# Choosing per sequence which states' dt*u*B TensorE makes, and issuing a step's two scans together

## The chip, the cores and the metric

The kernel runs on one core of a Trainium2 chip. Its time is the time that the device takes for one launch, in microseconds. The core has five engines that run side by side, each with its own queue of instructions: TensorE (PE in the profile; its weight loads are listed apart as PEld), VectorE (DVE), ScalarE (ACT), GpSimd (POOL) and SyncE (SP, which issues most of the DMAs here). All data is float32.

## What is computed

Two layers are applied to 16 sequences of 512 tokens with 256 channels. The first is a bidirectional selective state space layer with a residual and a layer norm; the second is a mixture of experts with soft slots (16 experts of 64 slots), again with a residual and a layer norm. The change touches the first only. Cut to what matters, with 512 inner channels and 16 states:

```python
xr = x @ in_proj_w.T                       # x part and gate "res"
xf = silu(causal_conv(xf));  xb = silu(causal_conv_b(xf))
# for each direction: delta (softplus), B and C come from u = xf or xb
dA = einsum('bld,dn->bldn', dt, A)
dB_u = einsum('bld,bld,bln->bldn', dt, u, B)          # dt*u*B
dA_cum = exp(reversed cumulative sum of the shifted dA)
xs = cumsum(dB_u * dA_cum, 1) / (dA_cum + 1e-12)
y = einsum('bldn,bln->bld', xs, C) + u * D            # times silu(res)
out = (y + y_b) @ out_proj_w.T
```

The kernel computes the running sum as a first order recurrence, h = exp(dt*A) * h + dt*u*B, and puts the division by (dA_cum + 1e-12) into a factor 1 + tanh(...). So for each sequence, direction, channel and state n there are: a product dt*u*B_n, a decay exp(dt*A_n), a tanh factor, one scan over the 512 positions, the product of scan and factor, and the product with C_n, summed over n.

## The kernel before, in words

The 512 inner channels stand on partitions as four chunks of 128; a tile is 128 channels by 512 positions. `seq_layers` goes through the sequences b. Each has four calls of `scan_part(b, r, p, ...)`: direction r (0 forward, 1 backward) and pair of chunks p, in the order (0,0), (1,0), (0,1), (1,1). A part walks through the 16 states two at a time (n and n+1) and for each through its two chunks. One state pair of one chunk is called a step here: 16 steps per part, 64 per sequence, 1,024 in all.

In a step:

- POOL makes `db` = du * B for the two states (line 427), from `du` = dt*u and from `bs`, two rows of B that a DMA spreads over all partitions (line 416).
- ACT writes exp(dt*A) into a PSUM bank `h` (line 444) and the tanh factor into `th` (line 446), for each of the two states.
- DVE scans in place in `h` (lines 450 and 452) and multiplies by (1 + `th`) into one half of `hg` (line 455).
- POOL multiplies `hg` by `cs`, the spread rows of C (line 456).
- PE adds `hg` into an accumulator by transposing it (`add_up`, line 371), two steps later.

For the states in DIAG, before the change 5 and 13, PE makes the product instead of POOL. `project_unit` writes the row of B_n onto the diagonals of four 128 by 128 blocks in DRAM (`diag_dram`, line 297, issued by ACT), with four clearing writes of `blank` at the start (line 188). `scan_part` loads those blocks as `dg` (line 420, on SP, a single buffer), `turn_pair` transposes `du` into `duT` once per part (lines 350 and 355), and `by_diagonal` multiplies the two into a PSUM bank `hd` (line 405), one step ahead of its use. Such a step has k = 1: `bs` and `db` hold one state only, and the decay of the other goes to `dec` in SBUF.

These buffers are small rings: `h` three banks, `th` three, `db` three, `bs` and `cs` three, `hg` four, `dec` two, and three further PSUM banks for everything else that PE does (`bank`), `hd` included.

Work beside the scan is cut into pieces by generators, held in three queues: `prep` (the next part's projections and step sizes: `pin`, `px`, `pz`, `pres`, `pdu`), `front` (finishing the former sequence and its dispatch to the slots: `pyt`, `po`, `pl`, `pd`, `pq`) and `back` (the experts of two sequences, `pg`, `pu`, `peo`, and `combine`, `cl`, `ctp`, `cpo`). `back` gets work from sequence 3 on, in the odd sequences, spread over 128 steps; in the last one over 64. After each step `beside_scan` lets the queues issue pieces, as long as no more than three banks are in use: `diags` holds the count of banks at each waiting `hd`, and `piece` stops when the count since the oldest one is over `BANKS`. `paced_piece` gives front and back a credit per step. What is left of front is issued at a sequence's end (`front.drain`, line 1023), what is left of back after the last sequence (`side_by_side`).

The order in which an engine's instructions stand in its queue is made by a planner when the program is built: of the instructions whose inputs and buffers it expects to be ready, it takes the one that comes first in the program. Instructions wrapped in `late` keep their place in the program's order.

Of the kernel before, what the change touches and what calls it, by code (L numbers as in the profile page):

```python
# [12 lines left out]
ALU = mybir.AluOpType  # L13
# [4 lines left out]
P = 128  # L18
# [6 lines left out]
NS = 16  # L25
DTR = 16
XB, XC = 32, 64
XW = XC + NS
KW = 4
NE = 16  # L30
DIAG = (5, 13)
DIAG_SIZE = P * (P + 1)
SL = 64
NSL = NE * SL
# [21 lines left out]
def seq_layers(tc, ident, neghalf, a, out):  # L56
# [20 lines left out]
    nc = tc.nc  # L77
    nb = a["x"].shape[0]
    with ExitStack() as ctx:
# [6 lines left out]
        diag_dram = drams.tile([2, len(DIAG), NL, DIAG_SIZE], F32, name="diag_dram")  # L86
# [176 lines left out]
        def prep_gate(b, fwd, out):  # L263
# [8 lines left out]
                late(nc.vector.scalar_tensor_tensor(res[:, c, :], res[:, c, :], 1.0, pp, ALU.add, ALU.mult))  # L272
            out["res"] = res

        def project_unit(b, r, out):

            w = side[r]
            q = f"{b}_{r}"
            yield GAP + 1
            px = bank(f"px_{q}")  # L280
            for c in range(ND):
                nc.tensor.matmul(
                    px[:XW, :], w["xT"][:, c, :], out["u"][:, c, :], start=(c == 0), stop=(c == ND - 1)
                )
            yield HOLD
            xd = p1.tile([XW, L], F32, tag=f"xd_{r}", name=f"xd_{q}")
            bc = dram.tile([2, NS, L], F32, tag="bc", name=f"bc_{q}")
            if r == 0:
                late(nc.scalar.activation(xd, px[:XW, :], AF.Identity, bias=unit))
            else:  # L290

                late(nc.scalar.activation(xd[: XB + NS, :], px[: XB + NS, :], AF.Identity, bias=unit[: XB + NS]))
                nc.scalar.copy(xd[XC:XW, :], px[XC:XW, ::-1])
            nc.sync.dma_start(bc[0], xd[XB : XB + NS, :])
            nc.sync.dma_start(bc[1], xd[XC:XW, :])
            step = DIAG[1] - DIAG[0]
            nc.scalar.dma_start(
                diag_dram[r].rearrange("i l (p s) -> i l p s", p=P)[:, :, :, 0],
                xd[XB + DIAG[0] : XB + NS : step, :].rearrange("i (l p) -> i l p", p=P),
            )  # L300
            out.update(xd=xd, bc=bc)

        def prep_pair(b, r, p, v):
# [88 lines left out]
        def scan_part(b, r, p, v, accs, done, then):  # L392

            prep.drain()
            prep.gens += [[1, g] for g in [turn_pair(b, r, p, v)] + then]
            w = side[r]
            made = {}

            def by_diagonal(n, c):

                diags.append(count[0])
                made[n, c] = h = bank(f"hd_{b}_{r}_{n}_{c}")
                for lc in range(NL):
                    s = slice(lc * P, (lc + 1) * P)
                    ins = nc.tensor.matmul(h[:, s], v[c][3][:, s], dg[:, s], start=True, stop=True)  # L405
                    if lc == 0:
                        late(ins)

            chunks = (2 * p, 2 * p + 1)
            for n in range(0, NS, 2):  # L410
                q = f"{b}_{r}_{p}_{n}"
                k = 1 if n + 1 in DIAG else 2

                bs = p4.tile([P, 2, L], F32, tag="bs", name=f"bs_{q}")
                cs = p4.tile([P, 2, L], F32, tag="cs", name=f"cs_{q}")
                nc.sync.dma_start(bs[:, :k, :], v["bc"][0, n : n + k, :].unsqueeze(0).to_broadcast([P, k, L]))
                nc.sync.dma_start(cs, v["bc"][1, n : n + 2, :].unsqueeze(0).to_broadcast([P, 2, L]))
                if n + 3 in DIAG:
                    dg = p4.tile([P, L], F32, tag="dg", name=f"dg_{q}", bufs=1)
                    nc.sync.dma_start(  # L420
                        dg.rearrange("p (l s) -> p l s", l=NL),
                        diag_dram[r, DIAG.index(n + 3), :, : P * P].rearrange("l (p s) -> p l s", p=P),
                    )
                for c in chunks:
                    dt, rr, du = v[c][:3]
                    db = p4.tile([P, 2, L], F32, tag="db", name=f"db_{q}_{c}")
                    nc.gpsimd.tensor_tensor(  # L427
                        db[:, :k, :], du.unsqueeze(1).to_broadcast([P, k, L]), bs[:, :k, :], ALU.mult
                    )
                    hg = p4.tile([P, 2, L], F32, tag="hg", name=f"hg_{q}_{c}", bufs=4)  # L430
                    hs = {}
                    for j in range(2):
                        if j < k:
                            dec = h = ps_h.tile([P, L], F32, tag="h", name=f"h_{q}_{c}_{j}")
                            hs[j] = (h, dec, db[:, j, :])
                        else:
                            h = made.pop((n + j, c))
                            dec = p4.tile([P, L], F32, tag="dec", name=f"dec_{q}_{c}", bufs=2)
                            hs[j] = (h, dec, h)

                    ths = {}
                    for j in range(2) if k == 2 else (1, 0):
                        s = slice(n + j, n + j + 1)
                        nc.scalar.activation(hs[j][1], dt, AF.Exp, scale=w["A"][:, c, s])  # L444
                        ths[j] = p4.tile([P, L], F32, tag="th", name=f"th_{q}_{c}_{j}")
                        nc.scalar.activation(ths[j], rr, AF.Tanh, bias=LN_1E12 / 2, scale=w["Ah"][:, c, s])  # L446
                    for j in range(2):
                        (h, dec, add), th = hs[j], ths[j]
                        if r == 0:
                            nc.vector.tensor_tensor_scan(h, dec, add, 0.0, ALU.mult, ALU.add)  # L450
                        else:
                            nc.vector.tensor_tensor_scan(  # L452
                                h[:, ::-1], dec[:, ::-1], add[:, ::-1], 0.0, ALU.mult, ALU.add
                            )
                        nc.vector.scalar_tensor_tensor(hg[:, j, :], th, 1.0, h, ALU.add, ALU.mult)  # L455
                    nc.gpsimd.tensor_tensor(hg, hg, cs, ALU.mult)  # L456
                    pending.append(
                        (r == n == 0, n == 0, r == 1 and n == NS - 2, c, hg, accs, w, v["u"], f"acc_{q}_{c}", done)
                    )
                    evict()  # L460

                    nxt_n = n if c == chunks[0] else n + 2
                    if nxt_n + 1 in DIAG:
                        for x in sides:
                            x.take_up()
                        by_diagonal(nxt_n + 1, chunks[1] if c == chunks[0] else chunks[0])
                    beside_scan()
                    if k == 1:
                        diags.pop(0)
                    add_up(2)  # L470
# [68 lines left out]
        prep, front, back = sides = [Side(), Side(), Side()]  # L539
# [556 lines left out]
```

## Time and profile before

| | us |
|---|---|
| median of 3 runs | 5415.38 (5413.15 to 5421.7) |
| the profiled execution | 5411.23 |
| its span, first to last instruction | 5409.4 |
| POOL busy | 4732.1 (87%) |
| DVE busy | 4559.7 (84%) |
| PE busy | 4331.1 (80%) |
| ACT busy | 4087.2 (76%) |
| first `hg` of the first sequence starts | 51.4 |
| last `hg` of the last sequence ends | 5132.3 |

Busy time is the time in which an engine executed at least one instruction; register and semaphore instructions and the issuing of DMAs are not counted. In a group's line of the profile stand the line of the kernel, the engine, the operation, what it writes and reads with shapes, the number of instructions; then their busy time and the mean of one in ns; then the idle time of the engine just ahead of them and what ended it. In a line of waits stand who waited for whom, the microseconds in all, how often, and the longest. A timeline's line has the start, the length, the engine and the instruction, and in brackets the idle time before it.

### The profile page before, as it was taken

The numbers are of one execution on the slowest core, as the hardware profiler recorded it, in microseconds if no ns is written. First come the engines' busy times: TensorE is split into PE (matmuls) and PEld (weight loads), VectorE is DVE, ScalarE is ACT, GpSimd is POOL, SyncE is SP. The second block draws the span as 40 slices with busy tenths as digits, with TensorE's granted clock in tenths as the row PEclk, the third lists the DMA queues.
The fourth block names the chain that finished last, engine by engine and source line by source line (L and its number), as shares of the span: only waits on it lengthen the run. The fifth ranks groups of instructions, "written<-read, shape, count | busy, mean of one in ns | idle before, by whom it ended". The sixth has DMA issues, their size and how long they took to land. (4 is left out here: it accounts for less than half of the span.)

```text
span 5409.4 us, 73721 instructions
## 1 busy us (share of the span) xinstructions
PE 4331.1 (80%) x24144; PEld 3390.0 (63%) x24145; DVE 4559.7 (84%) x6276; ACT 4087.2 (76%) x6515; POOL 4732.1 (87%) x2537
## 2 busy tenths in 40 slices
PE   5656666898888978788888977889787897888889
PEld 3445555676666666677656765667656776667657
DVE  7888988889898899888998888988899889988722
ACT  6677777787888778887877887788788887877641
POOL 6999999999999899998999989998999989988600
PEclk7778778898899988899888989899889998989999
DMA  4334333575446644566446754467444764457436
GB/s 137 131 117 137 125 129 131 189 230 159 156 142 212 225 149 148 158 223 213 131 144 194 232 170 153 132 212 232 149 149 146 225 224 134 145 179 234 126 103 188
DMA packets 595236, 907.73 MB, mean 168 GB/s; under 512 B 78082, under 2 KB 384898, under 8 KB 594852
## 3 DMA queue, kind: packets, MB, share of 16 engines
q1 hardware_dynamic: 521156, 859.87, 49.5%
q10 hardware_dynamic: 73696, 43.14, 2.8%
q8 instruction: 192, 3.15, 0.2%
q14 instruction: 192, 1.57, 0.1%
HBM read 840.86 MB, written 62.01 MB: 167 GB/s over the span
## 5 line engine op out<-in xcount | busy, mean ns | idle before, releaser
L456 POOL TENSOR_TENSOR hg<-hg,cs 128x1024 f32<-128x1024 f32 x1024 | 2420.8, 2368 | 128.1 <-DVE hg L455 110.0
L427 POOL TENSOR_TENSOR db<-du,bs 128x1024 f32<-128x1024 f32 (+1 forms) x1024 | 2144.4, 2098 | 232.3 <-DVE h L450 84.7
L371 PE MATMUL acc<-ident,hg 128*128 128x128 f32 x8192 | 1179.3, 295 | 203.3 <-POOL hg L456 181.6
L455 DVE SCALAR_TENSOR_TENSOR hg<-th,h 128x512 f32<-128x512 f32 x1792 | 1185.8, 678 | 177.2 <-PE acc L371 90.4
L371 PEld LDWEIGHTS acc<-ident,hg 128*128 128x128 f32 x8192 | 1044.9, 154 | 390.8 <-POOL hg L456 240.9
L452 DVE TENSOR_TENSOR_SCAN h<-h,db 128x512 f32<-128x512 f32 x896 | 1072.8, 1218 | 112.2 <-ACT h L444 107.5
L450 DVE TENSOR_TENSOR_SCAN h<-h,db 128x512 f32<-128x512 f32 x896 | 1071.1, 1217 | 48.8 <-ACT h L444 45.7
L446 ACT ACTIVATE th<-rr,Ah_f 128x512 f32<-128x512 f32 x1024 | 725.0, 714 | 186.3 <-DVE hg L455 183.1
L446 ACT ACTIVATE th<-rr,Ah_b 128x512 f32<-128x512 f32 x1024 | 721.5, 712 | 155.2 <-DVE hg L455 147.7
L444 ACT ACTIVATE h<-dt,A_f 128x512 f32<-128x512 f32 x896 | 608.2, 680 | 117.5 <-DVE hg L455 112.6
L444 ACT ACTIVATE h<-dt,A_b 128x512 f32<-128x512 f32 x896 | 608.6, 681 | 108.8 <-DVE hg L455 105.1
L687 PE MATMUL pl<-x2T,seT 128*128 128x512 f32 x512 | 299.1, 715 | 78.7 <-DVE hg L455 37.4
L405 PE MATMUL hd<-dg,duT 128*128 128x128 f32 x2048 | 305.6, 298 | 32.7 <-ACT yt L627 13.5
L830 PEld LDWEIGHTS pg<-st,Wg 128*128 128x128 f32 x2048 | 244.8, 196 | 106.2 <-issue 85.0
L405 PEld LDWEIGHTS hd<-dg,duT 128*128 128x128 f32 x2048 | 283.1, 214 | 38.4 <-ACT yt L627 15.7
L806 PE MATMUL peo<-Wd,ht 128*128 128x256 f32 x1024 | 257.0, 407 | 55.6 <-DVE rr L337 38.6
L779 PE MATMUL pu<-st,Wu 128*128 128x128 f32 x2048 | 254.5, 283 | 50.1 <-DMA Wu<-in_Wu_dram 32.7
L962 PE MATMUL cpo<-ceo,ct 128*128 128x256 f32 x1024 | 254.8, 407 | 46.9 <-DVE rr L337 39.9
L779 PEld LDWEIGHTS pu<-st,Wu 128*128 128x128 f32 x2048 | 244.9, 198 | 61.5 <-DVE h L452 24.2
L830 PE MATMUL pg<-st,Wg 128*128 128x128 f32 x2048 | 269.9, 286 | 4.1 <-DMA Wg<-in_Wg_dram 3.1
L884 PE MATMUL cl<-seT,cx 128*128 128x512 f32 x512 | 244.7, 617 | 32.5 <-DVE res L272 12.3
L806 PEld LDWEIGHTS peo<-Wd,ht 128*128 128x128 f32 x1024 | 205.3, 206 | 97.7 <-DVE rr L337 41.2
(154 smaller groups left out, 6654.8 us busy)
## 6 DMA issues: line engine op xcount, KB each, us to landing
cs<-bc SPq DMA_DIRECT2D x512, 512.0 KB, 3.9
bs<-bc SPq DMA_DIRECT2D x384, 512.0 KB, 5.1
Wg<-in_Wg_dram SPq DMA_DIRECT2D x128, 512.0 KB, 6.0
Wu<-in_Wu_dram SPq DMA_DIRECT2D x128, 512.0 KB, 6.0
Wd<-in_Wd_dram SPq DMA_DIRECT2D x128, 512.0 KB, 5.5
dg<-diag_dram SPq DMA_DIRECT2D x128, 256.0 KB, 4.2
bs<-bc SPq DMA_DIRECT2D x128, 256.0 KB, 3.6
x<-in_x_dram SPq DMA_DIRECT2D x32, 512.0 KB, 6.3
```

The source lines that it names most:

```text
L371: ins = nc.tensor.matmul(accs[c][:, s], hc[:, j, s], ident, is_transpose=True, start=False, stop=(last and j == 1 and lc == NL - 1),)
L405: ins = nc.tensor.matmul(h[:, s], v[c][3][:, s], dg[:, s], start=True, stop=True)
L427: nc.gpsimd.tensor_tensor(db[:, :k, :], du.unsqueeze(1).to_broadcast([P, k, L]), bs[:, :k, :], ALU.mult)
L444: nc.scalar.activation(hs[j][1], dt, AF.Exp, scale=w["A"][:, c, s])
L446: nc.scalar.activation(ths[j], rr, AF.Tanh, bias=LN_1E12 / 2, scale=w["Ah"][:, c, s])
L450: nc.vector.tensor_tensor_scan(h, dec, add, 0.0, ALU.mult, ALU.add)
L452: nc.vector.tensor_tensor_scan(h[:, ::-1], dec[:, ::-1], add[:, ::-1], 0.0, ALU.mult, ALU.add)
L455: nc.vector.scalar_tensor_tensor(hg[:, j, :], th, 1.0, h, ALU.add, ALU.mult)
L456: nc.gpsimd.tensor_tensor(hg, hg, cs, ALU.mult)
L779: nc.tensor.matmul(pu[:, fc * P : (fc + 1) * P], got["Wu", e][:, k, fc * P : (fc + 1) * P], st[:, k, :, j * SL : (j + 1) * SL], start=(k = ...
L806: nc.tensor.matmul(po[:, j * DM : (j + 1) * DM], ht[:, fc, :], got["Wd", e0 + j][:, fc, :], start=(fc == 0), stop=(fc == NF - 1),)
L830: nc.tensor.matmul(pg[:, fc * P : (fc + 1) * P], got["Wg", e][:, k, fc * P : (fc + 1) * P], st[:, k, :, j * SL : (j + 1) * SL], start=Fals ...
```

## The change

A function `diag_of(b)` chooses the states by sequence: 3, 7, 11 and 15 in sequences 0 to 2, states 3 and 11 in sequences 3 to 14, none in sequence 15. Everything that asked for DIAG asks for it now: the diagonal write, the load of `dg`, `by_diagonal`, and `turn_pair`, which is left out where there are no such states. `diag_dram` has room for four states, so eight clearing writes are issued at the start in place of four. Since state n+1 = 3 is in the second pair, `dg` is loaded in the first pair of a part (it was the second pair). Apart from that, the loop that issued scan, product, scan, product for the two states of a step issues scan, scan, product, product.

```diff
-DIAG = (5, 13)
+DIAG = (3, 7, 11, 15)
...
+        def diag_of(b):
+
+            return DIAG if b < 3 else DIAG[::2] if b + 1 < nb else ()
...
-            step = DIAG[1] - DIAG[0]
-            nc.scalar.dma_start(
-                diag_dram[r].rearrange("i l (p s) -> i l p s", p=P)[:, :, :, 0],
-                xd[XB + DIAG[0] : XB + NS : step, :].rearrange("i (l p) -> i l p", p=P),
-            )
+            ds = diag_of(b)
+            if ds:
+                step = ds[1] - ds[0]
+                own = diag_dram[r, DIAG.index(ds[0]) :: DIAG.index(ds[1]) - DIAG.index(ds[0])]
+                nc.scalar.dma_start(
+                    own.rearrange("i l (p s) -> i l p s", p=P)[:, :, :, 0],
+                    xd[XB + ds[0] : XB + NS : step, :].rearrange("i (l p) -> i l p", p=P),
+                )
...
-            prep.gens += [[1, g] for g in [turn_pair(b, r, p, v)] + then]
+            ds = diag_of(b)
+            prep.gens += [[1, g] for g in ([turn_pair(b, r, p, v)] if ds else []) + then]
...
-                k = 1 if n + 1 in DIAG else 2
+                k = 1 if n + 1 in ds else 2
...
-                if n + 3 in DIAG:
+                if n + 3 in ds:
...
                     for j in range(2):
-                        (h, dec, add), th = hs[j], ths[j]
+                        h, dec, add = hs[j]
                         if r == 0:
                             nc.vector.tensor_tensor_scan(h, dec, add, 0.0, ALU.mult, ALU.add)
...
-                        nc.vector.scalar_tensor_tensor(hg[:, j, :], th, 1.0, h, ALU.add, ALU.mult)
+                    for j in range(2):
+                        nc.vector.scalar_tensor_tensor(hg[:, j, :], ths[j], 1.0, hs[j][0], ALU.add, ALU.mult)
...
-                    if nxt_n + 1 in DIAG:
+                    if nxt_n + 1 in ds:
```

## The prediction

> **What bounds the kernel now.** I read the page's busy shares first, then the same shares in 40 slices of the span.
>
> ```profile
> PE 4331.1 (80%) x24144; PEld 3390.0 (63%) x24145; DVE 4559.7 (84%) x6276; ACT 4087.2 (76%) x6515; POOL 4732.1 (87%) x2537
> ...
> PE   5656666898888978788888977889787897888889
> ...
> POOL 6999999999999899998999989998999989988600
> ```
>
> POOL leads nearly everywhere; PE has room in the first seven slices only. The kernel has several regimes, so I cut it: 64 products `hg` (line 456, POOL) per sequence mark the borders. The view of busy time by window, for sequences 1, 4, 5, 15 and for what follows the scans:
>
> ```profile
> core 0: us, PE busy (x) PEld busy (x) DVE busy (x) ACT busy (x) POOL busy (x), PEclk, DMA share, GB/s
> ...
> 352.00:651.00 299.00, 200.59 (x1046) 158.39 (x1044) 262.67 (x322) 226.30 (x360) 292.70 (x153) 0.81 0.40 130
> ...
> 1276.00:1584.00 308.00, 244.41 (x1283) 185.28 (x1283) 282.13 (x384) 248.70 (x417) 295.27 (x157) 0.88 0.45 140
> 1584.00:1914.00 330.00, 285.01 (x1735) 230.51 (x1734) 283.77 (x398) 261.14 (x397) 294.92 (x156) 0.93 0.66 211
> ...
> 4765.00:5132.00 367.00, 310.76 (x1816) 248.85 (x1815) 282.35 (x414) 263.26 (x412) 285.22 (x150) 0.92 0.59 188
> 5132.00:5409.00 277.00, 248.69 (x1249) 185.01 (x1248) 67.52 (x191) 77.30 (x153) 14.96 (x45) 0.97 0.46 142
> ```
>
> Sequences 0 to 2 (301, 299, 300 us) are POOL's: 98% busy. From 3 on, POOL's work is the same, but its idle time grows with PE's load: 6 us at 201 us of PE, 13 at 244 (even sequences), some 33 at 285 (odd, which hold the experts), 82 at 311 in the last. After 5132 us PE sets the pace (249 of 277).
>
> What one product costs, from the groups kept apart by shape:
>
> ```profile
> L456 POOL TENSOR_TENSOR hg<-hg,cs 128x1024 f32<-128x1024 f32 x1024 | 2420.8, 2368 | 128.1 <-DVE hg L455 110.0 <-PE cpo L962 5.8 <-issue 4.3
> L427 POOL TENSOR_TENSOR db<-du,bs 128x1024 f32<-128x1024 f32 x768 | 1816.5, 2370 | 175.4 <-issue 66.3 <-DVE h L450 57.2 <-DVE h L452 42.2
> ...
> L427 POOL TENSOR_TENSOR db<-du,bs 128x512 f32<-128x512 f32 x256 | 327.9, 1281 | 57.0 <-DVE h L450 27.5 <-DVE h L452 15.0 <-POOL hg L456 11.4
> ```
>
> A state made by TensorE saves POOL 2.370 - 1.281 = 1.089 us per step. In the last sequence POOL waits for others; its waits there:
>
> ```profile
> POOL hg L456 <- DVE hg L455: 39.4, 17, 6.3
> POOL db L427 <- DVE h L450: 22.2, 7, 6.6
> ```
>
> And the start, from the timeline, where diag_dram is cleared and filled:
>
> ```profile
> 8.15 1.28 ACT L230 ACT_TABLE_LOAD   x1 [8.15 <-DMA diag_dram<-blank]
> ...
> 34.97 1.23 ACTq L297 DMA_DIRECT2D diag_dram<-xd  x1
> ...
> 46.81 0.37 SPq L420 DMA_DIRECT2D dg<-diag_dram  x1
> ```
>
> **The Trainium skill.** "Perfetto Trace Analysis", Optimization Strategy, says the most-contended engine can change over time; the windows agree. "GPSIMD Engine Reference", 4.1, rates a two-input elementwise operation about twice slower there than on VectorE and gives GPSIMD no way into PSUM: the trace has 2.37 us for 1024 elements, and TensorE's product is indeed read by VectorE's scan alone. "PSUM — Partial Sum Buffer", Engine vs sequencer instructions: queues are strict FIFO and matmuls keep program order; agrees, an `hd` matmul stands behind an `acc` that waits for POOL (in sequence 1 PE waits 45.2 us so). "DMA: Bandwidth & Descriptors", Rules for kernel authors: a strided last dimension becomes one descriptor per element; agrees, a diagonal write shows as 1,024 packets of 4 bytes, 9.6 us long at the start, 4.6 to 6.2 in sequences 0 to 3 after that.
>
> **The change, part by part.**
>
> *Sequences 0 to 2, four states.* Per sequence 16 more of the 64 steps save 1.089 us: 17.4 us of POOL, 293 to 276. Added: 16 `hd` groups on PE at 0.53 us (two take 1.06 in the timeline) = 8.5 us, on a PE at 67%; the exponential goes to SBUF (0.71 against 0.68 us), 0.5 us on ACT. VectorE stays at 263. So POOL 276, VectorE 263: no longer 30 us apart. The even sequences have VectorE at 92% and POOL at 96%; POOL 276 at 96% is 287.5. That is 12.5 less than 300, times three: -37.5. Ends: -17 each (idle as now), -7 each (VectorE bound, 263 at 90%).
> The bank bookkeeping: a waiting `hd` occupies one of three banks. Stepping the rule of take_up, piece and paced_piece through 64 steps, bank by bank, front's last piece still comes in step 12 of the fourth part in both versions, and no drain has leftovers: no cost. SP: `dg` has one buffer, so with a load every fourth step SP stands until the former `hd` is done, with the next `bs` and `cs` behind it; that `bs` is needed two steps (8.7 us) later and lands in 5.1, so POOL's lead hides it. Without that lead, up to 4 us per part, 48 in all.
>
> *Start.* Eight clearing writes stand in ACT's queue in place of four. The fourth now goes at 7.75 us, after the first landed, and ACT's first copy follows. Four more: +4 (0 to 7). The diagonal write has 2,048 elements: at the rate of 9.6 us per 1,024, about 10 us more, and `dg` is wanted two steps earlier than now. The third step's scan, at 55.4 us now, would wait until about 66 against 59 (shifted by 4): +7 (0 to 10). Together +11. Later writes are issued 40 to 55 us ahead of their reader: hidden.
>
> *Sequences 3 to 14, states 3 and 11 for 5 and 13.* POOL's work is equal. But the paced pieces shift. Stepping the rule, with each bank priced from the timeline (`pg` 3.1, `pu` 1.9, `peo`, `cpo` and `pq` 3.6, `cl` 1.8 us), the old setting gives 49 us more PE work in odd than in even sequences (measured 41). The new one lets more experts slip into the even ones: odd 285 to 267, even 244 to 262. POOL's idle is convex in PE's load (slope 0.15 below 244, 0.48 above): evening out is worth about 1.5 us each, over ten sequences -14; in four even ones a `pd` is left to front's drain, +5. So -9.
>
> *The last sequence and the end.* Removed: 16 `hd` (8.5 us) and eight `pdu` (4.4) on PE, eight copies on ACT. Added: 16 x 1.089 = 17.4 us on POOL, 285 to 303. With no bank held, pieces come earlier: by the rule seven of the eight last combine blocks fall here instead of five (the trace shows `cl` in five places before 5132 us), and two are carried in from sequence 14. A block is 3.6 + 1.1 + 3.6 = 8.3 us of PE. PE: 311 - 13 + 33, less ordering, about 324 to 331. At today's 85% share that is +15 or more, but the `hd` waits and bank holds are gone: +6 (-10 to +17). The end loses two blocks, 16.6 us at 90% busy, partly beside a chain: -12 (-18 to -4). POOL's added work hides in its 82 idle microseconds; were that cover gone, +17. Sum -6.
>
> *Two scans first.* No instruction more or less. The scan and its product run back to back without a gap already (median start to start 1.137 us, two scans 1.115), and in order of time two scans already follow one another 587 times in 1,024 steps. A gain: a product that waits for PE's `acc` (90.4 us in all) no longer holds the second scan, so `db` is free up to 1.1 us earlier. A loss: the first `h` bank and `th` come free one scan, 1.115 us, later, and ACT already waits 217.7 and 330.8 us for them; what is late next is the following exponential. No row prices the balance: I take 0, -25 to +25.
>
> Sum: -37.5 + 11 - 9 - 6 + 0 = -41.5 against the profiled execution, 5411.2 us (span 5409.4). The median of the runs shown, 5415.4, is 4 above it; so 5415.4 - 41.5 = 5374.
>
> **Rivals.** *VectorE takes over:* in the first sequences its 263 us with bursts of `taps` and waits for `hd` (17 us in sequence 1, twice as many `hd` now) leave only some 5 us each; -15 + 11 - 9 - 6 = -19, about 5396. For: 92% would be its highest share; against: `hd` waits are POOL's lateness seen from VectorE, and shrink with it. *More than I count:* the first three at -17, the start hidden, the scans' order helping odd sequences by 3 each: -51 + 3 - 18 - 15 = -81, 5334. *Slower:* `h` and `th` released later starve the scans of exponentials in the twelve PE-heavy sequences. The other gains are 41.5 us; over 768 steps 0.054 us lost per step cancels them, 5% of the later release. At 0.09 us: +69 - 41.5, about 5443. For: the existing ACT waits; against: ACT is 80% busy and POOL has VectorE's 26 idle us of an even sequence as slack. *No effect of the order:* the planner might place the same order; then its 0 holds and the first sum stands.
>
> **Chances.** Mine 0.56 (own range 5350 to 5398), VectorE 0.16, more 0.14, slower 0.14. Below 0.2% (11 us) a measurement of this kernel tells nothing. 0.07 of VectorE's case and 0.03 of mine end within that: faster 0.53 + 0.09 + 0.14 = 0.76, same 0.10, slower 0.14. The range leaves out the slower case alone: VectorE's with the order's +25 ends at about 5421, "more" with the order's best at about 5312; so 5312 to 5424.
>
> **What would show it.** Right: sequences 0 to 2 at 284 to 292 us, 288 half-width and 736 full `db` in all, odd and even sequences drawing together, fewer `cl` after the scans, ACT's first load near 12 us. Wrong: ACT's waits for `hg` and VectorE's for `h` grown by tens of us in sequences 3 to 14, or `hd` waits doubled with POOL idle in the first three.

## The result, and the profile after

The changed kernel takes 5468.05 us (median of 4 runs, 5456.52 to 5473.21) against 5416.43 us of the kernel before on the same chip: a ratio of 1.0092 [1.0076, 1.0108]. It is slower by 0.9%, where 5374 us and "faster" were forecast, and it lies above the forecast range. The profiled execution took 5468.9 us (span 5467.1).

The page of the changed kernel, busy shares and slices:

```profile
span 5467.1 us, 74299 instructions
PE 4379.9 (80%) x24345; PEld 3443.8 (63%) x24369; DVE 4559.7 (83%) x6276; ACT 4144.5 (76%) x6555; POOL 4702.2 (86%) x2537
...
PE   5667777887778878788887887788788787788889
...
POOL 6999999989989899988999889898898988988800
```

POOL does 29.9 us less than before, as it should, and yet is idle for 87.6 us more. VectorE's work is unchanged to the tenth. ScalarE has 57.3 us more to do, where the forecast had 1.5 us more and eight copies less.

The view of busy time by window, for the same stretches as before the change (sequences 1, 4, 5, 15, and what follows the scans; span of the window first, then PE, PEld, DVE, ACT, POOL):

```profile
336.00:621.00 285.00, 207.40 (x1176) 169.78 (x1176) 261.18 (x322) 225.80 (x361) 276.30 (x153) 0.83 0.45 137
1231.00:1541.00 310.00, 241.76 (x1256) 182.56 (x1257) 278.87 (x377) 246.90 (x410) 295.14 (x157) 0.89 0.46 139
1541.00:1877.00 336.00, 283.23 (x1672) 228.01 (x1673) 284.52 (x397) 266.84 (x406) 295.86 (x157) 0.92 0.62 197
4820.00:5190.00 370.00, 315.88 (x1777) 252.10 (x1779) 288.81 (x434) 261.00 (x420) 302.61 (x151) 0.93 0.59 188
5190.00:5467.00 277.00, 243.49 (x1209) 179.64 (x1206) 65.40 (x185) 74.88 (x147) 15.24 (x45) 0.94 0.45 142
```

The first sequences do what was forecast: POOL 276 us, and 285 us in place of 299. The middle and the end do not. Cut at every 64th `hg` product, the two traces give, in us:

| stretch | before | after | measured | forecast |
|---|---|---|---|---|
| start, to the first `hg` | 51.4 | 59.3 | +7.9 | +11 |
| sequences 0 to 2 | 900 | 848 | -52 | -37.5 |
| sequences 3 to 14 | 3813 | 3912 | +99 | -9 |
| sequence 15 | 368 | 370 | +2.9 | +6 |
| after the scans | 277 | 277 | -0.5 | -12 |

The forecast's sixth term, 0 for the order of the scans, has no stretch of its own; it lies in all of these. The loss is in the middle: odd sequences went from 1962 to 2015 us, even ones from 1851 to 1897. From 5 to 14 the odd ones now have 280 us of PE work each (284 before) and the even ones 255 (244): they did draw together, and both kinds grew longer.

The groups by shape show that the change does what it says: 288 half-width products and 736 full ones.

```profile
L465 POOL TENSOR_TENSOR hg<-hg,cs 128x1024 f32<-128x1024 f32 x1024 | 2420.3, 2365 | 193.5 <-DVE hg L464 114.4 <-issue 24.4 <-DVE m_mv L52 13.4
L435 POOL TENSOR_TENSOR db<-du,bs 128x1024 f32<-128x1024 f32 x736 | 1740.2, 2366 | 144.7 <-issue 53.5 <-DVE h L458 40.7 <-DVE h L460 21.9
...
L435 POOL TENSOR_TENSOR db<-du,bs 128x512 f32<-128x512 f32 x288 | 367.9, 1278 | 90.2 <-DVE h L460 31.2 <-issue 25.1 <-DVE h L458 22.2
```

The idle time ahead of `hg` is up from 128.1 to 193.5 us. Two of POOL's waits in the last sequence, which answer to those shown of before:

```profile
POOL hg L465 <- DVE hg L464: 31.5, 16, 4.3
...
POOL db L435 <- DVE h L458: 4.0, 2, 3.6
```

They are smaller now (39.4 and 22.2 before; the wait for the backward scan went from 4.7 to 6.6), so POOL is not held up more by the scans there. The start, from the timeline:

```profile
12.07 1.28 ACT L230 ACT_TABLE_LOAD   x1 [12.07 <-DMA diag_dram<-blank]
...
41.60 1.25 ACTq L304 DMA_DIRECT2D diag_dram<-xd  x1
...
51.30 0.37 SPq L428 DMA_DIRECT2D dg<-diag_dram  x1
...
56.88 2.50 POOL L435 TENSOR_TENSOR db<-du,bs 128x512 f32<-128x512 f32 x2 [4.31 <-DMA bs<-bc]
```

ACT's first load stands 3.9 us later, as worked out (+4); the rest, forecast at +7, came to +4. It came by another way than forecast: the diagonal write of 2,048 elements took 7.3 us from its first packet to its last, less than the 9.6 us of the 1,024 before. But the load of `dg` stands in SyncE's queue ahead of the next `bs`; SyncE waits 7.0 us for the diagonals, and POOL then 4.31 us for that `bs`.

Over the whole program, these waits of and for ScalarE changed most (waiting engine, for whom: us in all, times, longest):

```profile
ACT h L452 <- DVE hg L464: 274.0, 320, 5.2
ACT th L454 <- DVE hg L464: 201.5, 178, 3.9
DVE hg L464 <- ACT th L454: 142.2, 63, 8.8
```

The last of them, before the change:

```profile
DVE hg L455 <- ACT th L446: 40.2, 36, 5.9
```

And ScalarE waits less for VectorE's `hg` than before in the first two together (475 us against 548). So in some places ScalarE itself comes late, by up to 8.8 us. The experiments had to say which of the two edits does that, and by what.

### The profile page after: what moved, and what is told of

It reads as the page before. It is cut to its first block, busy times and chain, and to the rows that moved or that the text cites. A ratio compares the mean times of both kernels' runs of the same rounds, so it can differ in the third digit from the quotient of the medians.

```text
span 5467.1 us, 74299 instructions
## 1 busy us (share of the span) xinstructions
PE 4379.9 (80%) x24345; PEld 3443.8 (63%) x24369; DVE 4559.7 (83%) x6276; ACT 4144.5 (76%) x6555; POOL 4702.2 (86%) x2537
## 4 chain that ended last, share of the span: by engine, by line
DVE 28%; PE 21%; ACT 18%; issue 10%; POOL 3%; DMA 1%; DVEq 0%; ACTq 0%; SPq 0%; POOLq 0%
DVE h L458 7%; DVE hg L464 7%; DVE h L460 6%; ACT th L454 4%; ACT h L452 4%; PE pg L839 3%; PE acc L378 2%; PE pq L728 2%; PE cpo L971 2%; ACT L452 2%; PE cl L893 1%; PE pu L788 1%; PE pg L834 1%; DVE hd L458 1%; POOL hg L465 1%
## 5 line engine op out<-in xcount | busy, mean ns | idle before, releaser
L465 POOL TENSOR_TENSOR hg<-hg,cs 128x1024 f32<-128x1024 f32 x1024 | 2420.3, 2365 | 193.5 <-DVE hg L464 114.4
L435 POOL TENSOR_TENSOR db<-du,bs 128x1024 f32<-128x1024 f32 (+1 forms) x1024 | 2108.1, 2060 | 234.9 <-issue 78.6
L464 DVE SCALAR_TENSOR_TENSOR hg<-th,h 128x512 f32<-128x512 f32 x1760 | 1163.5, 682 | 262.1 <-ACT th L454 110.8
L458 DVE TENSOR_TENSOR_SCAN h<-h,db 128x512 f32<-128x512 f32 x880 | 1064.9, 1225 | 106.9 <-ACT h L452 102.4
L460 DVE TENSOR_TENSOR_SCAN h<-h,db 128x512 f32<-128x512 f32 x880 | 1057.6, 1222 | 64.8 <-ACT h L452 54.1
L413 PE MATMUL hd<-dg,duT 128*128 128x128 f32 x2304 | 374.4, 315 | 120.0 <-ACT duT L362 50.5
L413 PEld LDWEIGHTS hd<-dg,duT 128*128 128x128 f32 x2304 | 340.3, 227 | 139.0 <-ACT duT L362 57.8
L839 PEld LDWEIGHTS pg<-st,Wg 128*128 128x128 f32 x2048 | 265.4, 209 | 110.2 <-issue 84.4
L839 PE MATMUL pg<-st,Wg 128*128 128x128 f32 x2048 | 291.1, 300 | 1.6 <-DMA st<-s_dram 1.5
L728 PE MATMUL pq<-dis,xn 128*128 128x256 f32 x1024 | 255.4, 406 | 14.1 <-ACT ct L923 4.0
L696 PE MATMUL pl<-x2T,seT 128*128 128x512 f32 x512 | 250.6, 613 | 13.3 <-ACT sl L738 12.8
L815 PE MATMUL peo<-Wd,ht 128*128 128x256 f32 x1024 | 239.6, 387 | 25.1 <-DVE ht L800 15.1
```

Of the source, the lines that this page charges most:

```text
L435: nc.gpsimd.tensor_tensor(db[:, :k, :], du.unsqueeze(1).to_broadcast([P, k, L]), bs[:, :k, :], ALU.mult)
L460: nc.vector.tensor_tensor_scan(h[:, ::-1], dec[:, ::-1], add[:, ::-1], 0.0, ALU.mult, ALU.add)
L464: nc.vector.scalar_tensor_tensor(hg[:, j, :], ths[j], 1.0, hs[j][0], ALU.add, ALU.mult)
L728: nc.tensor.matmul(pq[:, k * 256 : (k + 1) * 256], xn[:, lc, k * P : (k + 1) * P], dis[:, lc, :], start=(lc == 0), stop=(lc == NL - 1),)
L839: nc.tensor.matmul(pg[:, fc * P : (fc + 1) * P], got["Wg", e][:, k, fc * P : (fc + 1) * P], st[:, k, :, j * SL : (j + 1) * SL], start=Fals ...
```

## The experiments

Each kernel was measured beside runs of the kernel before. Where runs that did not share a chip are compared, the differences below are those of the ratios, times 5415 us. "Scans first" is the new order of issue, "old order" the former one.

**One edit at a time.** The order alone, on the kernel before:

```diff
                     for j in range(2):
-                        (h, dec, add), th = hs[j], ths[j]
+                        h, dec, add = hs[j]
...
-                        nc.vector.scalar_tensor_tensor(hg[:, j, :], th, 1.0, h, ALU.add, ALU.mult)
+                    for j in range(2):
+                        nc.vector.scalar_tensor_tensor(hg[:, j, :], ths[j], 1.0, hs[j][0], ALU.add, ALU.mult)
```

> The kernel before with the two scans ahead of the two products; states 5 and 13 everywhere. Theory order (banks h and th come free one scan later, so ACT's exponentials and tanh factors come late in the PE-heavy sequences): sequences 3 to 14 lose the 99 us that the changed kernel lost there, ratio to before about 1.015 to 1.02, and ACT's waits for hg change as in the changed kernel (h up, th down). Theory states (states 3 and 11 in the middle sequences do it): within 0.3% of before, sequences 3 to 14 unchanged at about 3810 us in sum.

Measured: 5438.83 us, ratio 1.0052 [1.0036, 1.0068]: 28 us slower, between the two theories. The states alone are the changed kernel with these lines turned back:

> The changed kernel with scan, product, scan, product as before; only the states differ from before. Theory order: sequences 3 to 14 back at about 3810 us, sequences 0 to 2 keep some 44 us of gain, total about 0.7 to 0.9% faster than before. Theory states (at the start of a part hd waits for duT, and PE's queue behind it): the loss in sequences 3 to 14 stays near 99 us, total 0.8 to 1.0% slower than before, and the waits of hd for duT stay near 50 us.

Measured: 5422.51 us, 1.002 [1.0013, 1.0028]. Neither edit is a gain by itself as made, and against e2 the new order costs 39 us in the changed kernel. So there are two faults, both in sequences 3 to 14: e2 loses 75 us there against before (3888 against 3813), having won 55 in the first three and 10 in the last; e1 loses 24 there (3837).

**The middle sequences keep 5 and 13.** All else as in the change (only the place of the diagonals in `diag_dram` follows the new list), in the old order and then with scans first:

```diff
-            return DIAG if b < 3 else DIAG[::2] if b + 1 < nb else ()
+            return (3, 7, 11, 15) if b < 3 else (5, 13) if b + 1 < nb else ()
```

> Four states in sequences 0 to 2, states 5 and 13 in 3 to 14 as before, none in the last; scan, product, scan, product as before. Both theories: the middle as before, the gain of sequences 0 to 2 kept: about 5370 us, 0.8% faster than before. If it is not faster than 5400, neither the order nor the states 3 and 11 made the loss, and it comes from the earlier or the last sequences' changes carried on.

Measured: 5345.98 us, 0.9879 [0.9864, 0.9894].

> As the kernel with states 5 and 13 in the middle sequences, but with the two scans ahead. Theory order: the middle loses some 99 us, total near 5468. Theory states: no loss in the middle, near 5370. In between: each has a share, and the difference to the same kernel with the old order is the order's share at states 5 and 13.

Measured: 5379.45 us, 0.9944 [0.9929, 0.9959]. So the ideas for the first three sequences and for the last are worth 65 us together; states 3 and 11 in the middle cost 76 (e2 against e3) and the order 33 (e4 against e3). By stretches e3 differs from the profiled execution before by +4, -53, -3, -11 and 0 us.

**Which state does it.** One of the pair changed at a time, old order; against e3:

```diff
-            return (3, 7, 11, 15) if b < 3 else (5, 13) if b + 1 < nb else ()
+            return (3, 7, 11, 15) if b < 3 else (3, 13) if b + 1 < nb else ()     # e5
+            return (3, 7, 11, 15) if b < 3 else (5, 11) if b + 1 < nb else ()     # e6
```

> Old order of scan and product, four states in sequences 0 to 2, none in the last; the middle has states 3 and 13. Only the first of the two moved states differs from the kernel with 5 and 13 in the middle (5346 us). Theory start of a part (hd stands ahead of duT there and holds PE's queue): most of the 76 us loss is here, 5400 to 5425. Theory pacing (front's and back's pieces meet the doubled take_up at other places): somewhere between 5346 and 5425, not tied to state 3.

> As the kernel with 5 and 13 in the middle, with states 5 and 11. Theory start of a part: no loss, 5346 within 10 us, since the first group stays where it was. Theory pacing: a part of the 76 us, above 5360, as the second group meets other pieces.

Measured: 3 and 13 gave 5466.12 us, 1.0098 [1.0083, 1.0113], 119 us worse than 5 and 13; 5 and 11 gave 5328.93 us, 0.9844 [0.9822, 0.9866], 19 us better. State 3 does it: in place of 5 it costs 119 us beside 13 (more than either expectation had) and 95 beside 11 (e2 against e6). It isn't the number of products by TensorE, which is equal in all four.

**Why state 3.** `by_diagonal` is preceded by a loop that takes up whatever the three queues of pieces hold; `beside_scan`, called right after it, takes up again. A generator that stands at the mark WAIT is moved on by each take-up, so in a step with `by_diagonal` two waits pass at once. `finish` has two of them between the factors of the layer norm, which POOL works out, and the scaling by them:

```
            rs, sh = factors(mv, "m1")        # POOL: m_rs, m_sh
            ...
            yield WAIT
            yield WAIT
            scaled(xt, xt, sh, rs)            # ACT: four activations, the first of them `late`
```

The `by_diagonal` of state 3 is issued in a part's second and third steps, that of state 5 two steps later. The timeline of e2, sequence 8, part (1, 0), where `finish` stands at these marks just then, and they pass too early:

```profile
2605.36 0.23 POOL L607 TENSOR_SCALAR m_rs<-m_mv 128x4 f32<-128x4 f32 x1
...
2607.49 2.08 ACT L615 ACTIVATE x<-x,m_sh,m_rs 128x256 f32<-128x256 f32 x4 [5.62 <-POOL m_sh L610]
2609.47 0.49 ACT L667 ACTIVATE xn<-x,m_r 128x256 f32<-128x256 f32 x1
...
2611.22 0.71 ACT L454 ACTIVATE th<-rr,Ah_b 128x512 f32<-128x512 f32 x1
...
2611.96 0.69 DVE L463 SCALAR_TENSOR_TENSOR hg<-th,h 128x512 f32<-128x512 f32 x1 [4.68 <-ACT th L454]
```

ACT stands 5.62 us in front of `x`, whose factors POOL begins 3.5 us into that stand, because its `db` and `hg` come first; the tanh factor is queued behind it, behind four `xn` as well, and VectorE waits 4.68 us for that, POOL after it. The Trainium skill, "PSUM — Partial Sum Buffer", Engine vs sequencer instructions, says that ScalarE's queue is strict FIFO. This trace agrees (the tanh factor starts as the last `xn` ends, at 2611.22), and here it turns a scaling that nobody needs yet into a stop for everybody. The waits in sequences 5 to 14, first e2, then e3:

```profile
DVE hg L463 <- ACT th L454: 113.0, 41, 8.0
...
ACT x L615 <- POOL m_sh L610: 44.0, 10, 5.6
```

```profile
ACT x L615 <- POOL m_sh L610: 25.1, 10, 4.0
DVE hg L463 <- ACT th L454: 21.2, 25, 1.4
```

The same ten scalings wait 19 us longer, and VectorE 92 us longer for the tanh factor. In the even sequences from 6 to 14 the first four steps of that part take 24.5 us in e2 and 20.7 in e3. e5, which also has state 3, shows the long waits for `m_sh` as well (96.4 us in the whole execution, 49.0 in e3), and e6, without it, does not (56.1). But VectorE's wait for the tanh factor is only 60.5 us in all of e5, which is slower than e2, so this stop alone doesn't make e5 slow.

Then the test: keep 3 and 11, and take the second take-up away, first for front and back as a whole, then only for a queue that stands at WAIT.

```diff
                     if nxt_n + 1 in ds:
-                        for x in sides:
+                        for x in sides if b < 3 else (prep,):
                             x.take_up()
```

> States 3 and 11 in the middle, old order; from sequence 3 on only prep, not front and back, is taken up ahead of a step's hd, so front's and back's waits take one step each as elsewhere. Theory doubled take_up (two of front's marks pass in one step at a bad place, so that ACT stands at an instruction that POOL has not fed yet): most of the 76 us comes back, near 5360. Theory start of a part: no change against states 3 and 11 with the full take_up, 5422 within 10 us.

```diff
                         for x in sides:
-                            x.take_up()
+                            if b < 3 or not x.wait:
+                                x.take_up()
```

> States 3 and 11 in the middle, old order (5422 us); ahead of hd all sides are taken up as in the changed kernel, but from sequence 3 on not one that stands at a WAIT mark, so such marks take one step each. Theory WAIT (two WAIT marks pass in one step, and the residual's scaling and norm come to ACT in one clump, before POOL has made their factors): most of the 52 us that taking up prep alone gave come back, near 5370. Theory banks held: it stays near 5422.

Measured: 5370.79 us, 0.9921 [0.9904, 0.9938], and 5375.73 us, 0.9923 [0.9907, 0.994]. They give back 54 and 53 of the 76 us, and VectorE's wait for the tanh factor falls from 137.9 us in the whole of e2 to 33.0 and 34.7 (e2 and e16):

```profile
DVE hg L463 <- ACT th L454: 137.9, 55, 8.0
```

```profile
DVE hg L463 <- ACT th L454: 34.7, 44, 2.1
```

e16 changes nothing but the take-up at WAIT marks, so in the old order it is these marks, passed too early, that cost 53 us. By which ways was not taken apart. The stop shown above is one: with e16 its four steps take 22.3 us, 2.2 less than in e2, a small part of the 53. ACT's wait for `m_sh` falls only from 73.9 us to 64.8 in all; what is gone at that place is the tanh factor that stood behind it. The other theory, that `hd` stands in PE's queue for `duT` at the start of a part, expected no change from e7 and fell.

A second thing goes with it. In the groups of ACT's table loads, e2 first, then e3:

```profile
L858 ACT ACT_TABLE_LOAD x33 | 42.3, 1283 | 0.6
```

```profile
L858 ACT ACT_TABLE_LOAD x17 | 21.8, 1283 | 0.3
```

Line 858 is the second of two `ht` (Gelu) that used to follow one another; in 16 more places an exponential now stands between them. Over the whole program e2 loads tables 383 times and e3 335 times, and 48 times 1.283 is 61.6 us, all of ACT's added work (4138.6 against 4076.8 us). (The Trainium skill, "ScalarE activation tables: per-element evaluation and per-set limits", What a function is on this engine, has 1283 ns for a switch; this trace agrees.) e7 and e16 load 354 times. How the 53 us divide between standing ACT and loading ACT was not measured, and loads alone rank nothing: e5, as slow as the change itself, loads 323 times. The last 23 us of the 76 stay open; in e7 the odd sequences from 5 to 13 are 5 us longer each than in e3, their last part by 5 and the other three together by nothing, and the even ones are as long.

e5's further loss has another mark in the waits, of e5 and then of e3:

```profile
DVE res L1017 <- PE acc L378: 59.0, 25, 6.6
```

```profile
DVE res L1017 <- PE acc L378: 3.9, 7, 1.1
```

The gate product at a sequence's end waits for PE's last sums. By the counting rule, 3 and 13 leave `pl`, `pd` and `pq` to front's drain, which PE does ahead of them; 3 and 11 leave `pd` and `pq` in even sequences, 5 and 11 nothing. The traces agree: the last `pq` of an even sequence starts 13 us after the next sequence's first `hg` in e5 and 7 us after it in e2 (means of sequences 6 to 14), 2 us before it in e3, and 11 us before it in e6. This goes with the time of sequences 3 to 14: 3923, 3888, 3810 and 3791 us. In e7 and e16 it is 2 us after, so their edits moved this too, and it may be one of the ways to the 53 us, though VectorE's own wait for these sums falls only from 22.2 us in e2 to 18.9 and 16.9. No run takes it alone.

**Why the order costs.** Three suspicions. First, that the second scan waits for its exponential behind the first tanh; then issuing both exponentials ahead of both tanhs would make the new order free:

```diff
                         nc.scalar.activation(hs[j][1], dt, AF.Exp, scale=w["A"][:, c, s])
+                    for j in range(2) if k == 2 else (1, 0):
+                        s = slice(n + j, n + j + 1)
                         ths[j] = p4.tile(...)          # and the tanh
```

> States 5 and 13 in the middle, two scans first (5379 us with the old order on ACT), and ACT issues both exponentials ahead of both tanh factors. Theory queue (the second scan, now ahead of the first product, waits for an exponential that ACT makes only after a tanh): the order's 33 us come back, near 5346. Theory banks (h comes free one scan later, whatever ACT's order): no gain, 5379 or more.

Measured: 5339.44 us, 0.9861 [0.9846, 0.9876], 45 us better than e4. That looked like the answer, until the same edit was made under the old order:

> States 5 and 13 in the middle, scan, product, scan, product, but ACT issues both exponentials ahead of both tanh factors. Theory queue: with the old order the first product waits for a tanh that now comes third, as the second scan did for its exponential, so this is slower than 5346, by 10 to 40 us. If it is as fast as 5339, ACT's order alone gives the gain, whatever VectorE's order is.

Measured: 5314.3 us, 0.982 [0.9798, 0.9842]. That expectation was wrong: exponentials first gains 32 us there as well, and the new order still costs 22. So it is a gain by itself, and accounts for a third of the order's cost at most. Where that gain comes from was not found; 14 to 15 us of it can be table loads (326 against 338 in e8, 324 against 335 in e11).

Second, that a small copy into `xb`, which ACT does in the midst of a step, falls badly; it was given to VectorE under both orders (e4 and e3):

```diff
-   nc.scalar.copy(xb[:, c, 0 : KW - 1], pb[:, 0 : KW - 1])
+   nc.vector.tensor_copy(xb[:, c, 0 : KW - 1], pb[:, 0 : KW - 1])
```

> States 5 and 13 in the middle, two scans first (5379 us), with the copy of the three first columns of xb made by VectorE in place of ACT. Theory xb (the second scan now goes ahead of the last tap, ACT stands at the copy of xb for it, and the exponentials behind it come late): ACT's 45 us of waits for xb are gone and the order's 33 us come back, near 5350. Theory banks (h and th free one scan later everywhere): 5375 or more.

> The control: the same copy moved under the old order (5346 us), where ACT waits 4 us for it. Theory xb: no change beyond 10 us. If this gains as much as the new order does, the copy's place is worth something by itself and says nothing of the order.

Measured: 5380.9 us, 0.9935 [0.992, 0.995], and 5340.08 us, 0.9852 [0.9835, 0.987]. The order still costs 41 us, and that theory fell. (The control is 15 us faster than e3, where 10 at most were expected.)

Where the loss lies: in sequences 5 to 14, e4 against e3, most pairs of steps take the same time, and a few do not: counted from 0, in odd sequences steps 6 and 7 of the first part take 15.1 us against 10.9, steps 10 and 11 take 14.4 against 9.2. There ACT has a burst with table loads (in the second of the two it also waits 1.5 us for PE in e4). e4, sequence 9:

```profile
2855.18 1.28 ACT L259 ACT_TABLE_LOAD   x1
2856.47 1.91 ACT L259 ACTIVATE xb<-xb 128x2048 f32<-128x2048 f32 x1
...
2860.41 1.23 DVE L458 TENSOR_TENSOR_SCAN h<-h,db 128x512 f32<-128x512 f32 x1 [2.97 <-ACT h L452]
2861.04 1.28 ACT L856 ACT_TABLE_LOAD   x1
...
2865.53 1.23 DVE L458 TENSOR_TENSOR_SCAN h<-h,db 128x512 f32<-128x512 f32 x1 [3.09 <-ACT h L452]
```

A silu with its loads, then a Gelu with its loads, and VectorE stands twice, 2.97 and 3.09 us. In e3, at the same place, no exponential stands between the silu and the Gelu; one load is saved, and VectorE stands once:

```profile
2833.96 1.28 ACT L259 ACT_TABLE_LOAD   x1
2835.25 1.92 ACT L259 ACTIVATE xb<-xb 128x2048 f32<-128x2048 f32 x1
2837.19 1.28 ACT L855 ACT_TABLE_LOAD   x1
...
2841.68 1.23 DVE L458 TENSOR_TENSOR_SCAN h<-h,db 128x512 f32<-128x512 f32 x1 [3.43 <-ACT h L452]
```

And from the start of the silu's load VectorE has work for 4.3 us in e3 and for 2.3 us in e4. The waits of scans for exponentials in sequences 5 to 14, e3 and then e4:

```profile
DVE h L460 <- ACT h L452: 64.1, 63, 3.2
DVE h L458 <- ACT h L452: 33.4, 15, 3.4
```

```profile
DVE h L460 <- ACT h L452: 76.4, 66, 3.6
DVE h L458 <- ACT h L452: 71.9, 50, 3.1
```

51 us more. The third suspicion was the ring that sets this lead: `th`, of which each buffer is read a scan later, or the three banks of `h`. A fourth `th` buffer, under both orders (its room comes from the combine's `cm`):

```diff
-   ths[j] = p4.tile([P, L], F32, tag="th", ...)
+   ths[j] = p4.tile([P, L], F32, tag="th", ..., bufs=4)
-   cms = [p3.tile([P, 512], F32, tag="cm", ...) ...]      # and ct
+   cms = [p3.tile([P, 512], F32, tag="cm", ..., bufs=2) ...]
```

> e4_mid513_new with four buffers for the tanh factor instead of three (room comes from a ring of the combine, three to two). If the tanh ring is what shortens ScalarE's lead under the new order, this comes to within 10 us of e18 (the old order with four buffers), near 5345, and the wait of VectorE's product for the tanh factor and of the scan for the exponential fall back to the old order's. If the three banks of h do it, it stays 25 to 40 us above e18, near 5375.

> The control: e3_mid513_old with the same four buffers. Both theories expect little here, 5330 to 5350 (5346 without); the smaller ring of the combine could add up to 5.

Measured: 5385.17 us, 0.9948 [0.9933, 0.9963], and 5337.32 us, 0.9859 [0.9843, 0.9876]: still 48 us apart. A fourth buffer for `th` doesn't take the order's cost away. ACT's waits under the new order, e17:

```profile
ACT h L452 <- DVE hg L464: 305.1, 277, 7.0
...
ACT th L454 <- DVE hg L464: 98.4, 92, 2.9
```

With room in `th`, ACT stands in front of `h` instead (180.2 us in e4), but no longer than under the old order (in e18 the two are 328.9 and 120.0). The banks of `h` are what is left of the suspicions. That they are the cause was not shown, and a fourth bank was not tried. e17 also loads tables 356 times against 328 in e18, so up to 36 of its 48 us may be that. A rival stands untested: each edit lets the planner place the activations anew, as the silu and the Gelu above show, and no run kept ACT's queue as it was while VectorE's order changed. The cause of the order's cost stays open.

**The last sequence.** As e3, with 5 and 13 there too:

```diff
-            return (3, 7, 11, 15) if b < 3 else (5, 13) if b + 1 < nb else ()
+            return (3, 7, 11, 15) if b < 3 else (5, 13)
```

> Four states in sequences 0 to 2, states 5 and 13 in all others, the last included; old order. Against the kernel that has none in the last (5346 us): theory last sequence (no diagonal there is worth the 12 us that the last sequence fell by): 12 us more, about 5358, and the last sequence back at 368. Theory chance (the last sequence also fell to 357 when only the scans' order was changed, so its length depends on how pieces happen to fall): within 5 us of 5346.

Measured: 5370.51 us, 0.9922 [0.9902, 0.9941], 23 us worse than e3. Leaving them out at the end is a gain. By the traces, the last sequence takes 371 us with them and 356 without, at 314 and 295 us of PE; the two profiled executions differ by 16 us.

**Both repairs on the changed kernel, and the best of the parts.** The change with the edits of e7 and e8, exponentials first and a single take-up from sequence 3 on:

> The changed kernel (states 3 and 11 in the middle, two scans first) with both suspected causes taken away: both exponentials first, and only prep taken up ahead of hd from sequence 3 on. If the causes add (45 us for the order there, 52 us for the doubled take_up): 5468 - 97 = about 5371, faster than before by 0.8%. If it stays above 5440, one of the two causes was only a shift in the planner's order.

Measured: 5419.6 us, 1.0006 [1.0, 1.0013]: 47 us better than the change and 48 worse than expected. The gains of e7 and e8 do not add up. The even sequences came back to their time (1857 us), the odd ones did not (2027, the change 2015). VectorE's wait for the tanh factor is down to 22.4 us, and yet this kernel is 79 us slower than e8, which has 5 and 13 instead; without any repair the same step, from e4 to the change, costs 80. So the WAIT marks are shown to cost time in the old order only. With scans first, states 3 and 11 cost 79 us with both repairs and 80 with neither, no run there has one repair alone, and why stays open.

With e6's states, 5 and 11, and e8's exponentials first, with scans first (e10) and in the old order (e15):

> States 5 and 11 in the middle (5329 us with the old order), two scans first and both exponentials first. If the 40 us that issuing both exponentials first gave at states 5 and 13, against scans first alone, and the 17 us of states 5 and 11 are independent: about 5322. Theory leftovers (front has nothing left at a sequence's end with 5 and 11): odd sequences near 317 us again.

> States 5 and 11 in the middle, old order, both exponentials first: 5329 with ACT's old order, less the 32 us that both exponentials first gave at 5 and 13: about 5297 if independent, the fastest so far. If the new order cost nothing at 5 and 11, it equals the 5312 of the same kernel with the new order.

Measured: 5312.46 us, 0.9812 [0.9797, 0.9828], and 5310.37 us, 0.9804 [0.9788, 0.9821]. Both beat the kernel before by about 2% and the changed one by nearly 3%, and the order makes no difference that can be measured here. e15 stays 13 us above the 5297 of independent gains. The page of e15:

```profile
span 5306.7 us, 74211 instructions
PE 4341.5 (82%) x24352; PEld 3398.4 (64%) x24369; DVE 4522.3 (85%) x6276; ACT 4067.9 (77%) x6504; POOL 4700.3 (89%) x2537
```

POOL's work is that of the changed kernel to 2 us, its share 89% against 86%.

## Why the prediction was wrong

*Sequences 3 to 14, states 3 and 11 for 5 and 13: failed.* This is the step that failed first. It priced the move by PE's load alone ("evening out is worth about 1.5 us each") and gave -9; the states cost 76 (e2 against e3). Even the 1.5 us hang on a curve bent through three points: at the one slope that is given above 244 us, 18 us less in one sequence and 18 us more in the other cancel. Some of the evening out is there (odd and even sequences are 25 us of PE apart, 40.5 before; 5 was forecast), and it buys nothing. The idle time that grew with PE's load in the profile before went with it, but didn't follow it here: e6 and e3 have the same states in number and the same work and differ by 19 us. What the step left out was the code two lines above `by_diagonal`. Moving the product to another pair of steps moves a take-up of all three queues with it. I stepped that rule for the banks and counted the pieces that it lets out, but not the WAIT marks that it lets pass, nor what then stands in ACT's queue ahead of a tanh. In the old order the marks make 53 of the 76 us (e16). The other 23, and all of the 80 that the states cost with scans first, stay open.

*Two scans first: failed.* I took 0, with 25 either way; it costs 28 (e1), 33 (e4 against e3) and 39 (change against e2), just outside that range, and nothing at 5 and 11 with exponentials first. The "slower" rival named a loss that is there, scans that wait for exponentials (51 us more in e4), at +69. The rival's even loss per step was wrong: the order is nearly free in most steps and costs 3 to 5 us in the few pairs where ACT has table loads to do. "ACT is 80% busy", used against it, is an average that hides those bursts. Its later release of `th` is not borne out by a fourth buffer, that of `h` is neither shown nor excluded. The prediction also left out that the planner would place ACT's other work anew, as it does with the silu and the Gelu. (For two scans in a row the trace gives 1.133 us, not 1.115; nothing hangs on it.)

*Sequences 0 to 2: right, and mis-sized.* -37.5 forecast, -52 measured (23.7, 14.4 and 13.6 us). POOL's work came to the 276 us worked out, VectorE's stayed at 261, and POOL is at 99, 97 and 96%: VectorE did not take over, and this part was as large as the rival "more than I count" had it. Four fifths of the surplus are in sequence 0. The single `dg` buffer was said to be hidden, and POOL at these shares leaves no room for the 48 us that it could have cost.

*Start: right in size, half of it by another way.* +11 forecast, +7.9 measured, +4 of it the clearing writes. The other +4 is not the longer diagonal write, which was priced at about 10 us more and took 2.3 less, but the `bs` that waits behind it in SyncE's queue.

*Last sequence and end: the sum right, its parts not.* In the old order e3 gains 11 there (forecast 6), and e9 shows 23 for the removal by itself; by the two traces, which are 16 us apart, 15 of them lie in the last sequence. I expected that sequence to grow and the end to shrink by two combine blocks. The trace of the change has 80 `cl` matmuls after the scans against 88: one block, and the end is as long as before, 277 us. In the change the sequence lost its gain again (370 us, 357 in e2). The order alone doesn't do that: e4 has 356, and e5, in the old order, 370.

So the three terms that held came out better than forecast: start, first three and last part give -60 in e3, against -32.5 for the same terms. The two failed steps put 76 and 39 us on top. My reading of the bound, POOL by 98% in the first stretch, held where one engine was full. In the middle no engine is, and kernels with equal work there took from 3778 us (e15) to 3923 (e5). (The low end of the stated range, 5312, doesn't follow from its terms either: 5334 less 25 is 5309, and 5327 where the order's 18 are in it already.)

## What to carry to other kernels

When an edit moves an instruction to another step, list everything that the program does at that place, marks and hand-backs of side work included, and ask what each in-order queue then holds in front of the critical instruction. In a stretch where no engine is full (here POOL at 88 to 95%), don't price an edit by an engine's load: look at the bursts (table loads, groups of four activations) and at how many results the consumer has in hand when one begins. Count ScalarE's table loads before and after. A change of several parts wants a run per part: here 65 us of gain lay under 115 us of loss.

## What was not expected

The order of four activations within a step, exponentials before tanhs, is worth 45 us under the new order (e8 against e4), 32 under the old one (e11 against e3) and 22 with 5 and 11 (e15 against e6), with no instruction added. Moving both states by one pair of states, 5 to 3 and 13 to 11, made ScalarE load its tables 48 times more (1.283 us each) with no activation more on its queue, while moving either alone did not (323 and 333 loads, against 335). And the cost of the scans' order went from 33 us to nothing with two small edits elsewhere: such costs don't add.
